# One base for a pair of edge tiles and an untyped first block, in a relational graph layer

## The chip, the cores and the metric

The kernel runs on one core of a Trainium2 chip. The metric is device microseconds (us) of one execution. Three runs of the kernel before took 2129.83 to 2131.13 us, median 2130.83 us. The profiled execution took 2129.83 us.

## The reference

A residual block: rows are normalized and rectified, each edge carries the row of its source through the weight matrix of its type, and the results are summed by destination.

```python
h = jnp.maximum(_layernorm(x, axis=-1), 0.0)          # x: 12500 x 256
hx = jnp.einsum('ni,rio->rno', h, weight)             # 8 types, 256 x 256 each
msg = hx[edge_type, src]                              # 212500 edges
agg = jax.ops.segment_sum(msg, dst, num_segments=num_nodes)
out = x + agg * 0.5**0.5 + h_bias + (h @ loop_weight) * 0.5**0.5
```

The edges are sorted by destination, stably, from 100000 random pairs taken in both directions followed by 12500 self loops. So the last edge of every node is its self loop, and it has a random type like all others.

## The kernel before, in words

The kernel sums before it multiplies. For each node and each of the 8 types it adds up the rows h of the sources (`acc`, a ring of 6 slots of 128 nodes in SBUF, transposed: features on partitions, in two halves of 128 features), and then multiplies each 128 nodes, a *group*, by the eight weights and the loop weight (16 + 2 products, L808, two PE instructions each as the data are f32). There are 98 groups.

**Tiles.** A *unit* is a run of consecutive edges that lies in one partition of a block; a block has 128 units. In the kernel before a unit has 267 edges (`EDGES`). The last edge of each node is taken out of it by five compaction steps on VectorE (L338, L339), which leaves at most 256, two *tiles* of 128. There are 796 units, 1592 tiles and 7 blocks. GpSimd issues one indirect gather for each tile (L637): 128 source rows of 1 KB, from x for the first tiles (their rows are then normalized on the spot, the `e_` lines), from the stored h (`h32`) later. VectorE builds a one-hot matrix for four tiles at once (L650): edge by (node in a window, type). The window is 14 nodes (`WIN`), so 112 columns for a tile. TensorE multiplies (L674, 2 halves x 2 instructions for a tile), VectorE adds the 128 x 224 result to `acc` at a column that a register holds (L684, `add_sums`, one for each tile). Each tile has its own base, hence its own register and its own add.

**Last edges.** They come back by type: for each node the type of its last edge is found (`mark`, `find_types`, `spread_types`), and `begin(g)` writes, for each of the 8 types, the node's own transposed row where the type agrees and zero where it doesn't (8 instructions of L704). That also clears the slot of the ring. `begin` of the groups 0 to 5 stands in the first stage, in `norm_rows`; of the others in `finish` of the group that had the slot before.

**Order.** It is written out by hand. The loop over tiles t issues in each step the gather of tile t + 58 (`AHEAD`), pieces of the normalization of x to h32 in the first 28 or so steps (26 pieces, 4 before the loop, three in four steps), one-hots for later tiles, the edge products of t, steps of `background` work, group products by a budget, and the adds one unit late (`LAG`). Message buffers hold 62 tiles (`MSGS`). `prepare(b)` makes the indices, columns and offsets of block b; its some 70 VectorE instructions go to `background` from step 256 b - 300 on (`PREP`), three list entries (`OPS`) for every 3 steps (`STEP`). All engines run their queues in order. In the last block, which is not full, `load_indices` fills `nat_d` by an iota on GpSimd (L306) before the edges are loaded into it by SP, so this iota stands in GpSimd's queue behind the gather of tile t + 58, and VectorE's first step of the block (L348) waits for the load.

Of the kernel before, what the change touches and what calls it, by code (L numbers as in the profile page):

```python
# [31 lines left out]
WIN = 14  # L32
# [3 lines left out]
SLOTS = 6  # L36
RING = GROUP * SLOTS
# [3 lines left out]

# [19 lines left out]
PREP = 300  # L61
STEP = 3
# [5 lines left out]
class Plan:  # L68
# [5 lines left out]

    def __init__(self, N, E):
        U = EDGES / PAIR
        self.NU = NU = -(-E // EDGES)
        self.NT = NT = NU * PAIR - (1 if E - (NU - 1) * EDGES <= P else 0)
        slack = 6.5 * (E / 4) ** 0.5 / U + 1.0
        self.rate = rate = E / (N * U)  # L80

        self.low = [(1 / rate, -slack / rate), (1.1 / rate, -(2.0 + 0.1 * E / U) / rate)]
        self.high = [(1 / rate, slack / rate)]
        self.starts = list(range(0, N, GROUP))
        self.ends = self.starts[1:] + [N]
        self.NG = len(self.starts)
        self.last = [
            min([NT - 1, *(int((e + 2 - b) / a) + 1 for a, b in self.low)]) for e in self.ends]

        self.last = [min(NT - 1, t + (PAIR - 1 - t) % PAIR) for t in self.last]  # L90
        self.last[-1] = NT - 1

        a, b = self.high[0]
        self.blocks = [
            [k for k in range(-(-NU // P))
             if max(f * PAIR * P * k + o for f, o in self.low) <= e + 2
             and a * PAIR * min(NU - 1, P * k + P - 1) + b + WIN + LASTS + 2 >= s]
            for s, e in zip(self.starts[::XG], self.starts[XG::XG] + [N])]
        a, b = self.high[0]
        self.first = [max(0, int((s - WIN - 2 - b) / a) - 1) if s else 0 for s in self.starts]  # L100

# [101 lines left out]
def kernel(  # L203
# [16 lines left out]
    C = R * WIN  # L220
    assert PAIR * KC * C <= 512
# [5 lines left out]
    EU = E - (NU - 1) * EDGES  # L227
# [18 lines left out]
    low = const.tile([P, NB * PAIR], F32, name="low")  # L246
    high = const.tile([P, NB * PAIR], F32, name="high")
# [4 lines left out]
    ones_b = const.tile([P, P], BF16, name="ones_b")  # L252
    flag = const.tile([1, 1], I32, name="flag")
# [8 lines left out]
    with ExitStack() as main:  # L262
# [11 lines left out]

        selves = main.enter_context(tc.tile_pool(name="selves", bufs=SLOTS + 1))
        marks = main.enter_context(tc.tile_pool(name="marks", bufs=1))
# [14 lines left out]
        added, begun = {}, set()  # L291
# [3 lines left out]
        def load_indices(b):  # L295
            rows_ = min(P, NU - b * P)
            last = b == NB - 1
            full = rows_ - last
            e0 = b * P * EDGES
            nat = {}  # L300
            for name, a, more in (("s", src, 0), ("d", dst, 1), ("t", etype, 0)):
                n = ep.tile([P, EDGES + more], I32, name=f"nat_{name}")
                if last:

                    if more:
                        nc.gpsimd.iota(  # L306
                            n, pattern=[[2, EDGES + 1]], base=N - 2 * EU, channel_multiplier=0)
                    else:
                        nc.vector.memset(n, 0)
                if full:  # L310
                    nc.sync.dma_start(n[:full, :], bass.AP(
                        tensor=a.tensor, offset=a.offset + e0, ap=[[EDGES, full], [1, EDGES + more]]))
                if last:
                    nc.sync.dma_start(
                        n[full : full + 1, :EU], a[E - EU : E].rearrange("(p q) -> p q", p=1))
                nat[name] = n
# [17 lines left out]
        def compacted(got, bit, bits):  # L334

            def step(k):
                m = work_tile(got, "moves", 6, I32)
# [6 lines left out]
        def sources(b, got):  # L344


# [15 lines left out]
            def codes():  # L362
                nc.vector.scalar_tensor_tensor(
                    got["code"], got["code"], float(R), got["t"], op0=ALU.mult, op1=ALU.add)

            def packs():
                nc.vector.scalar_tensor_tensor(
                    packed, got["s"], float(1 << (TB + SB)), got["code"],
                    op0=ALU.mult, op1=ALU.add)

            def unpacks():
                nc.vector.tensor_single_scalar(
                    work_tile(got, "from", 6, I32)[:, :U], packed[:, :U], TB + SB,
# [11 lines left out]
        def last_edges(b, got):  # L385

            def selves_():
                nc.vector.tensor_tensor(
                    work_tile(got, "same", 4), got["s"], got["d"][:, :EDGES], op=ALU.is_equal)

            def ends():
                nc.vector.scalar_tensor_tensor(
                    work_tile(got, "end", 5), got["rise"], 1.0, got["same"],
# [7 lines left out]
            def codes():  # L401
                nc.vector.scalar_tensor_tensor(
                    got["rise"], got["rise"], -2.0 * R, got["t"], op0=ALU.mult, op1=ALU.add)
# [12 lines left out]
            def kept():  # L416
                nc.vector.tensor_single_scalar(
                    work_tile(got, "kinds", 6, I32)[:, :LASTS], packed[:, :LASTS], 2 * R - 1,
# [19 lines left out]
        def columns(b, got):  # L438


            two = slice(b * PAIR, (b + 1) * PAIR)

            def begins():
                got["begin"] = small.tile([P, PAIR], F32, name="begin")
                nc.vector.tensor_copy(got["begin"][:, 0:1], firsts[b])
                more = small.tile([P, 1], I32, name="more")
                nc.vector.tensor_single_scalar(
                    more, got["rest"][:, P : P + 1], TB, op=ALU.logical_shift_right)
                nc.vector.tensor_tensor(got["begin"][:, 1:2], firsts[b], more, op=ALU.add)

            def bases():
                got["base"] = small.tile([P, PAIR], F32, name="base")
                nc.vector.tensor_tensor(got["base"], got["begin"], low[:, two], op=ALU.max)
                nc.vector.tensor_tensor(got["base"], got["base"], high[:, two], op=ALU.min)

            def offs():
                got["off"] = small.tile([P, 1], F32, name="off")
                nc.vector.tensor_tensor(got["off"], firsts[b], got["base"][:, 0:1], op=ALU.subtract)
                got["add"] = small.tile([P, PAIR], F32, name="add")
                nc.vector.tensor_scalar(  # L460
                    got["add"], got["base"], firsts[b], float(-R), op0=ALU.subtract, op1=ALU.mult)
                nc.vector.tensor_scalar(got["add"], got["add"], 1.0, None, op0=ALU.add)
# [15 lines left out]
            def moved():  # L478
                work_tile(got, "col", 2)
                for i in range(PAIR):  # L480
                    h = slice(i * P, (i + 1) * P)
# [4 lines left out]
            def to():  # L486
                nc.vector.scalar_tensor_tensor(
                    got["there"][:, :U], got["col"][:, :U], float(C), got["there"][:, :U],
                    op0=ALU.is_le, op1=ALU.mult)
# [19 lines left out]
            return [begins, bases, offs, fits, number, there, moved, to, final, valid, sum_, all_,  # L509
                    *turned(got, "col", lambda: col.setdefault(b, cols.tile([P, U], F32, name="cols")))]  # L510

        def places(b, got):

            def wraps_():
                got["wrapped"] = small.tile([P, PAIR, NK], F32, name="wrapped")
                for i in range(PAIR):
                    nc.vector.tensor_scalar(
                        got["wrapped"][:, i, :], wraps, got["base"][:, i : i + 1], None,
                        op0=ALU.is_lt)

            def turns():
                got["turns"] = small.tile([P, PAIR], F32, name="turns")
                nc.vector.tensor_reduce(got["turns"], got["wrapped"], AX.X, ALU.add)

            def position():
                got["pos"] = small.tile([P, PAIR], F32, name="pos")
                nc.vector.scalar_tensor_tensor(
                    got["pos"], got["turns"], float(-RING), got["base"], op0=ALU.mult, op1=ALU.add)

            def turn():  # L530
                pt = ps_d.tile([P, 512], F32, tag="pt", name="ptr")
                for i in range(PAIR):
                    nc.tensor.transpose(
                        pt[0:1, i * P : (i + 1) * P], got["pos"][:, i : i + 1], ident)
                place[b] = small.tile([1, U], I32, name="offs")
                nc.vector.tensor_copy(
                    place[b].rearrange("o (u i) -> o i u", i=PAIR),
                    pt[0:1, :U].rearrange("o (i u) -> o i u", i=PAIR))
# [71 lines left out]
        def norm_rows(i):  # L610
# [4 lines left out]
            def rest():  # L615
                after()
                nc.sync.dma_start(rows_of(h32, i), xt[:n, :k, :])
                for g in range(d // P, min(d // P + k, SLOTS, plan.NG)):
                    begin(g, xt[:, g - d // P, :])
# [38 lines left out]
        def load_offsets(t0):  # L658
            n = min(REGS, NT - t0)
            b, q = divmod(t0, U)  # L660
# [3 lines left out]
            for i, v in enumerate(vals):  # L664
                offsets[t0 + i] = v

        def edge_sums(t):
            m, o = msg.pop(t), oh.pop(t)
            if t % PAIR == 0:
                bank = ps_e.tile([P, 512], F32, name="ps")  # L670
                sums["ps"] = bank[:, : PAIR * KC * C].rearrange("p (i c k) -> p i c k", i=PAIR, c=KC)
            ps = sums["ps"][:, t % PAIR]
            for c in range(KC):
                nc.tensor.matmul(ps[:, c], m[:, c * P : (c + 1) * P], o, start=True, stop=True)  # L674
# [5 lines left out]
        def add_sums(t, ps):  # L680
            a = acc[:, :, :, bass.ds(offsets.pop(t), WIN)]
# [3 lines left out]
            added[t] = i.ins  # L685

            assert all(g in begun for g in range(plan.NG) if plan.first[g] <= t)


        def begin(g, rows_):  # L690

            n = plan.ends[g] - plan.starts[g]
            pst = ps_d.tile([P, 512], F32, tag="pt", name="pst")
# [4 lines left out]
            got["self", g] = selves.tile([P, KC, GROUP], F32, name="self_t")  # L698
            copy = nc.scalar.activation(got["self", g][:, :, :n], pst[:, :, :n], AF.Copy)  # L699
            q, k = divmod(g, XG)  # L700
            of = typed[q][:, k * GROUP : k * GROUP + n].unsqueeze(1).to_broadcast([P, KC, n])
            s0 = g % SLOTS * GROUP
            for r in range(R):
# [3 lines left out]
                if r == 0:  # L707
                    tc.add_manual_dep(i.ins, copy.ins.name, SYNC_DEP, reason="one reader at a time")
            begun.add(g)
# [347 lines left out]
```

## Time and profile before

| what | value |
|---|---|
| profiled execution, span and time | 2128.1 us, 2129.83 us |
| median of three runs | 2130.83 us |
| busy: PE, DVE, POOL, ACT | 1642.2, 1475.9, 1515.6, 202.5 us |
| first gather, first edge product | 12.87 us, 81.86 us |
| last gather, last group product ends | 2098.2 us, 2123.1 us |
| first gather from h32 | 189.28 us |
| weights scaled by ACT | 194.8 and 198.7 us, 1.91 us each |
| mean granted clock of TensorE | 0.892 |

How to read it: PE is TensorE's products, DVE is VectorE, ACT is ScalarE, POOL is GpSimd, SP the queue of plain transfers. A view by groups has, after the count, the time in which such instructions ran, the mean of one in ns, and the idle time of the engine ahead of them with what ended it. In views by window the first number is the window's length in us; behind the engines stand the granted clock, the DMA engines' mean busy share and GB/s. A wait is told for the engine that stood still and for what it waited for.

### The profile page before, as it was taken

The numbers are of one execution on the slowest core, as the hardware profiler recorded it, in microseconds if no ns is written. First come the engines' busy times: TensorE is split into PE (matmuls) and PEld (weight loads), VectorE is DVE, ScalarE is ACT, GpSimd is POOL, SyncE is SP. The second block draws the span as 40 slices with busy tenths as digits, with TensorE's granted clock in tenths as the row PEclk, the third lists the DMA queues.
The fourth block names the chain that finished last, engine by engine and source line by source line (L and its number), as shares of the span: only waits on it lengthen the run. The fifth ranks groups of instructions, "written<-read, shape, count | busy, mean of one in ns | idle before, by whom it ended". The sixth has DMA issues, their size and how long they took to land.

```text
span 2128.1 us, 31245 instructions
## 1 busy us (share of the span) xinstructions
PE 1642.2 (77%) x10433; PEld 1497.1 (70%) x10433; DVE 1475.9 (69%) x4268; ACT 202.5 (10%) x473; POOL 1515.6 (71%) x1619
## 2 busy tenths in 40 slices
PE   1134799879999379998389998489999058999999
PEld 0123789769888369887379887378888047888897
DVE  7787887887777387776387776387776067777863
ACT  1465410000000000000000000000000000000000
POOL 6723677777777777777777777777777766777773
PEclk9855899989999699999699999699999578999999
DMA  4786344344434344434344434344344334434442
GB/s 132 234 278 200 87 135 144 105 134 136 135 106 143 104 135 135 137 105 142 105 135 134 131 110 142 105 135 136 106 134 137 104 95 122 135 107 134 131 119 67
DMA packets 145838, 279.32 MB, mean 131 GB/s; under 512 B 27924, under 2 KB 94732, under 8 KB 145676
## 3 DMA queue, kind: packets, MB, share of 16 engines
q0 software_dynamic: 76416, 208.77, 33.7%
q1 hardware_dynamic: 69260, 68.53, 10.1%
q8 instruction: 85, 1.39, 0.3%
q14 instruction: 77, 0.63, 0.1%
HBM read 251.59 MB, written 25.60 MB: 130 GB/s over the span
## 4 chain that ended last, share of the span: by engine, by line
PE 62%; DVE 17%; issue 10%; POOL 4%; DMA 3%; ACT 2%; DVEq 1%; SPq 0%; ACTq 0%; POOLq 0%
PE po L808 33%; PE ps L674 28%; DVE acc L704 5%; POOL msg L637 4%; DVE acc L684 3%; DMA msg<-h,gidx 2%; DVE moves L338 1%; DVE e_stats L585 1%; ACT xt L597 1%; PE pst L696 1%; DVE fixed L339 1%; DVE n_stats L585 1%; DVE oh L650 1%; ACT self_t L699 1%; PE ptt L731 1%
## 5 line engine op out<-in xcount | busy, mean ns | idle before, releaser
L637 POOL DMA_INDIRECT msg<-h,gidx x1496 | 1421.1, 950 | 489.6 <-issue 413.9
L674 PEld LDWEIGHTS ps<-oh,msg 128*128 128x128 f32 x6368 | 960.3, 201 | 372.1 <-issue 179.9
L674 PE MATMUL ps<-oh,msg 128*128 128x112 f32 x6368 | 961.2, 283 | 272.3 <-issue 96.3
L808 PE MATMUL po<-w,acc 128*128 128x256 f32 x3136 | 922.8, 398 | 0.8 <-DVE flag L551 0.8
L684 DVE TENSOR_TENSOR acc<-acc,ps 128x224 f32 x1592 | 613.1, 385 | 122.6 <-PE ps L674 77.3
L808 PEld LDWEIGHTS po<-w,acc 128*128 128x128 f32 x3136 | 529.5, 199 | 26.7 <-issue 0.8
L650 DVE TENSOR_TENSOR oh<-fixed,cols 128x448 f32<-128x448 f32 x398 | 246.8, 620 | 204.5 <-PE ps L674 173.0
L704 DVE SCALAR_TENSOR_TENSOR acc<-types,pst 128x256 f32<-128x256 bf16 (+1 forms) x784 | 267.7, 414 | 63.2 <-ACT self_t L699 60.2
L699 ACT ACTIVATE self_t<-pst 128x256 f32<-128x256 f32 x98 | 37.5, 382 | 1533.5 <-PE pst L696 1533.5
L637 POOL DMA_INDIRECT msg<-in_x_dram,gidx x96 | 92.2, 960 | 93.2 <-issue 57.3
L808 PE MATMUL po<-wl,self_t 128*128 128x256 f32 x392 | 119.6, 434 | 0.0
L808 PEld LDWEIGHTS po<-wl,self_t 128*128 128x128 f32 x392 | 75.4, 214 | 7.4
L731 PE MATMUL ptt<-loops,mark 128*128 128x24 bf16 x272 | 11.4, 178 | 85.8 <-DVE acc L704 83.6
L731 PEld LDWEIGHTS <-mark 128*128 128x128 bf16 x272 | 9.0, 100 | 95.2 <-DVE acc L704 89.2
L326 DVE CAST gidx<-ptr 128x256 int32<-128x256 f32 x7 | 2.9, 420 | 103.5 <-DMA msg<-h,gidx 101.1
L696 PE MATMUL pst<-ident,hr 128*128 128x128 f32 (+1 forms) x184 | 35.9, 278 | 35.4 <-DVE gidx L326 33.9
L348 DVE TENSOR_TENSOR rise<-nat_d 128x267 f32<-128x267 int32 x7 | 3.0, 433 | 79.7 <-DMA nat_d<-in_dst_dram 79.7
L597 ACT ACTIVATE xt<-xt,n_shift,n_rstd 128x256 f32<-128x256 f32 x98 | 51.0, 589 | 29.2 <-DVE n_shift L594 29.2
L597 ACT ACTIVATE msg<-msg,e_shift,e_rstd 128x256 f32<-128x256 f32 x96 | 49.7, 588 | 20.5 <-DVE e_shift L594 18.6
L696 PEld LDWEIGHTS pst<-ident,hr 128*128 128x128 f32 (+1 forms) x184 | 23.6, 151 | 35.8 <-DVE gidx L326 34.0
L819 DVE TENSOR_TENSOR xr<-xr,po 128x256 f32<-128x256 f32 x98 | 40.4, 412 | 8.2 <-PE po L808 7.4
L338 DVE TENSOR_SCALAR moves<-fixed 128x267 int32<-128x267 int32 x98 | 42.3, 432 | 2.1
(209 smaller groups left out, 459.9 us busy)
## 6 DMA issues: line engine op xcount, KB each, us to landing
msg<-h,gidx POOLq DMA_INDIRECT x1496, 2.7
xt<-in_x_dram SPq DMA_DIRECT2D x24, 512.0 KB
h<-xt SPq DMA_DIRECT2D x24, 512.0 KB
xr<-in_x_dram SPq DMA_DIRECT2D x24, 512.0 KB
out_dram<-xr SPq DMA_DIRECT2D x24, 512.0 KB
hr<-h SPq DMA_DIRECT2D x23, 512.0 KB
w<-in_L_gnn_weight_dram SPq DMA_DIRECT2D x2, 1024.0 KB
msg<-in_x_dram,gidx POOLq DMA_INDIRECT x96, 2.8
```

What stands on the lines that cost most here:

```text
L338: nc.vector.tensor_single_scalar(m, packed, 1 << (bit + k), op=ALU.bitwise_and)
L585: nc.vector.bn_stats(stats[:n, j, :], rows_[j])
L597: nc.scalar.activation(rows_[j], rows_[j], AF.Relu, bias=shift[:n, j : j + 1], scale=rstd[:n, j : j + 1])
L637: nc.gpsimd.indirect_dma_start(out=msg[t], out_offset=None, in_=table[:, :], in_offset=bass.IndirectOffsetOnAxis(ap=gidx[b][:, at : at + 1 ...
L650: nc.vector.tensor_tensor(o[:, k : k + v, :i, :], iota_f.unsqueeze(1).unsqueeze(1).to_broadcast([P, v, i, C]), of.unsqueeze(3).to_broadcas ...
L674: nc.tensor.matmul(ps[:, c], m[:, c * P : (c + 1) * P], o, start=True, stop=True)
L684: i = nc.vector.tensor_tensor(a, a, ps, op=ALU.add)
L696: nc.tensor.transpose(pst[:, c, :n], rows_[:n, c * P : (c + 1) * P], ident[:n, :n])
L699: copy = nc.scalar.activation(got["self", g][:, :, :n], pst[:, :, :n], AF.Copy)
L704: i = nc.vector.scalar_tensor_tensor(acc[:, :, r, s0 : s0 + n], of, float(r + 1), pst[:, :, :n], op0=ALU.is_equal, op1=ALU.mult)
L731: nc.tensor.matmul(pt[:, g, :], m[:, i, g * GROUP : (g + 1) * GROUP], loops[b][:, i, :], start=(b, m, i) == parts[0], stop=(b, m, i) == pa ...
L808: i = nc.tensor.matmul(got["out", g][:n], lhs, rhs, start=(r == R and c == 0), stop=(r == R - 1 and c == KC - 1))
```

## The change

- **First block.** Its units have 256 edges and keep all of them, self loops too. So its `sources` needs no compaction, it has no `last_edges`, and its columns come from the destinations themselves (`plain` and so on). The other blocks are as before, 267 edges in a unit. There are 802 units and 1603 tiles.
- **Groups of the first block.** The first three groups of four (`typed` = 3, so groups 0 to 11) lie in it wholly. For them no types are found and `begin` is not called: ScalarE clears the slot (`clear`, 2048 columns of zero), three slots ahead of the loop, three from `background`, the next six in `finish`; the node rows that the loop weight needs are turned later, when the group's turn comes (`turn_nodes` from a re-load of h32).
- **One base for a unit.** The window is 22 nodes for the unit; the first tile's one-hot reaches columns 0 to 22 of it (176 columns with the types), the second's 4 to 22 (144 columns). Both tiles add into one result in PSUM, 352 wide, and one add and one register serve the unit. One-hots are 176 wide for both tiles (704 for four).
- **Background.** `PREP` is 184 for 300 and `STEP` 2 for 3: block b is prepared from step 256 b - 184 on, three entries for every 2 steps. No block is prepared early; block 1 had begun at step 0.
- **Plan.** Due times are counted in units, by the two slopes of edges to units; an add waits for the clearing of a slot that it is the first to reach (`zeroed`).

```diff
-WIN = 14
+WIN = 22
+REACH = ((0, 22), (4, 18))
-PREP = 300
-STEP = 3
+PREP = 184
+STEP = 2
...
         def sources(b, got):
+            if b == 0:
+                def copy():
+                    nc.vector.tensor_copy(work_tile(got, "sf", 2)[:, :U], got["s"][:, :U])
+
+                return [copy, *turned(
+                    got, "sf", lambda: gidx.setdefault(b, idx.tile([P, U], I32, name="gidx")))]
...
         def last_edges(b, got):
+            if b == 0:
+                return []
...
-            return [begins, bases, offs, fits, number, there, moved, to, final, valid, sum_, all_,
+            if b == 0:
+                return [
+                    bases, plain, plain_from, plain_to, plain_typed, plain_final, plain_sum, *turned(
+                        got, "col", lambda: col.setdefault(b, cols.tile([P, U], F32, name="cols")))]
+            return [bases, offs, fits, number, there, moved, to, final, valid, sum_, all_,
...
             def rest():
                 after()
                 nc.sync.dma_start(rows_of(h32, i), xt[:n, :k, :])
-                for g in range(d // P, min(d // P + k, SLOTS, plan.NG)):
-                    begin(g, xt[:, g - d // P, :])
                 load_rows(i + ROWS - 2)
...
-                sums["ps"] = bank[:, : PAIR * KC * C].rearrange("p (i c k) -> p i c k", i=PAIR, c=KC)
-            ps = sums["ps"][:, t % PAIR]
+                sums["ps"] = bank[:, : KC * R * WIN].rearrange("p (c k) -> p c k", c=KC)
+            ps = sums["ps"]
+            i = t % PAIR
+            from_, width = (a * R for a in REACH[i])
+            end = t == NT - 1 or i == PAIR - 1
             for c in range(KC):
-                nc.tensor.matmul(ps[:, c], m[:, c * P : (c + 1) * P], o, start=True, stop=True)
+                nc.tensor.matmul(
+                    ps[:, c, from_ : from_ + width], m[:, c * P : (c + 1) * P], o[:, :width],
+                    start=(i == 0 and c == 0), stop=(end and c == KC - 1))
...
-        def add_sums(t, ps):
-            a = acc[:, :, :, bass.ds(offsets.pop(t), WIN)]
+        def add_sums(u, ps):
+            a = acc[:, :, :, bass.ds(offsets.pop(u), WIN)]
...
+        def clear(g):
+
+            s0 = g % SLOTS * GROUP
+            a = acc[:, :, :, s0 : s0 + GROUP].rearrange("p c r d -> p (c r) d")
+            i = nc.scalar.activation(a, zero.unsqueeze(2).to_broadcast([P, KC * R, GROUP]), AF.Copy)
+            zeroed[g, "slot"] = i.ins
+
+        def turn_nodes(g, pool):
 
             n = plan.ends[g] - plan.starts[g]
+            rows_ = got["h", g // XG][:, g % XG, :]
...
+        def begin(g):
+
+            n = plan.ends[g] - plan.starts[g]
             q, k = divmod(g, XG)
+            pst, copy = turn_nodes(g, selves)
...
                 if b < plan.NG:
-                    begin(b, got["h", b // XG][:, b % XG, :])
+                    if q < plan.typed:
+                        clear(b)
+                    else:
+                        begin(b)
...
-            background = []
-            early = {0}
-            for q in range(-(-min(SLOTS, plan.NG) // XG)):
-                for b in plan.blocks[q]:
-                    if b not in early:
-                        early.add(b)
-                        for f in prepare(b):
-                            f()
-                mark(q)
-                find_types(q)
-                spread_types(q)
+            for g in range(min(CLEARED, plan.NG)):
+                clear(g)
+
+            background = [(4 * (g - CLEARED), lambda g=g: clear(g))
+                          for g in range(CLEARED, min(SLOTS, plan.NG))]
...
                 for b in range(1, NB):
-                    if t == max(0, U * b - PREP) and b not in early:
+                    if t == max(0, U * b - PREP):
...
-                waiting.append((t, ps))
-                while waiting and (
-                        t == NT - 1 or t % PAIR == PAIR - 1 and len(waiting) > LAG * PAIR):
-                    for i in range(min(PAIR, len(waiting))):
-                        u, ps = waiting.pop(0)
-                        add_sums(u, ps)
+                if t % PAIR == PAIR - 1 or t == NT - 1:
+                    waiting.append((t // PAIR, ps))
+                while waiting and (len(waiting) > LAG or t == NT - 1):
+                    u, ps = waiting.pop(0)
+                    add_sums(u, ps)
```

## The prediction

> **What bounds the kernel now.** First the page's slices (span in 40, so 53.2 us each).
>
> ```profile
> PE   1134799879999379998389998489999058999999
> POOL 6723677777777777777777777777777766777773
> PEclk9855899989999699999699999699999578999999
> ```
>
> POOL shows 7 nearly throughout, while PE has holes, some down to 3 and one to 0. So the even engine is POOL, though no engine looks full. Next the groups, to see what POOL does, and the prices of what the change touches.
>
> ```profile
> L637 POOL DMA_INDIRECT msg<-h,gidx x1496 | 1421.1, 950 | 489.6 <-issue 413.9
> L674 PE MATMUL ps<-oh,msg 128*128 128x112 f32 x6368 | 961.2, 283 | 272.3 <-issue 96.3
> L684 DVE TENSOR_TENSOR acc<-acc,ps 128x224 f32 x1592 | 613.1, 385 | 122.6 <-PE ps L674 77.3
> L650 DVE TENSOR_TENSOR oh<-fixed,cols 128x448 f32<-128x448 f32 x398 | 246.8, 620 | 204.5 <-PE ps L674 173.0
> L704 DVE SCALAR_TENSOR_TENSOR acc<-types,pst 128x256 f32<-128x256 bf16 (+1 forms) x784 | 267.7, 414 | 63.2 <-ACT self_t L699 60.2
> ```
>
> A gather is 0.95 us and is followed by 0.30 us that nothing else explains. That is a cadence, and the gathers by window show it.
>
> ```profile
> 82.00:188.00 106.00, 39.37 (x42) 0.55 0.79 254
> 188.00:266.00 78.00, 42.76 (x46) 0.78 0.44 136
> 266.00:1640.00 1374.00, 1040.45 (x1096) 0.93 0.43 127
> ```
>
> From 266 to 1640 us POOL issued 1096 gathers in 1374 us, 1.25 each: it never stopped, and PE's holes there cost nothing. Before that it stopped: all 62 buffers were full while the normalization went on. Its lost time until the last block's iota: 1295 gathers stand ahead of that, 12.9 + 1295 x 1.25 = 1632, and the iota starts at 1714.2, so 82 us: by 188 us (97 gathers) 54, from 188 to 266 (46 gathers) 20, and 8 later.
>
> Then what happens at that iota (VectorE's and POOL's order of time).
>
> ```profile
> 1645.01 0.28 DVE L309 MEMSET nat_t<- 128x267 int32 x1
> 1716.46 0.44 DVE L348 TENSOR_TENSOR rise<-nat_d 128x267 f32<-128x267 int32 x1 [71.17 <-DMA nat_d<-in_dst_dram]
> ```
>
> ```profile
> 1714.22 0.37 POOL L306 IOTA nat_d<- 128x268 int32 x1
> ```
>
> PE had caught up with the gathers, VectorE reached step 1236 and then stood 71 us, because POOL's iota stands behind the gather of tile 1294. All engines but POOL stand with it. After it PE is the bound: 350 tiles (1242 of 1592 are done) end at 2123.1. From 1800 to 2100 the edge products count 1144, so 286 tiles in 300 us, 1.049 each; 350 x 1.049 = 367, and the other 40 of the 407 us are 25 in 1716 to 1800 (224 products, 56 tiles, in 84 us, block 6 being prepared) and 15 at the end. So the end is: **POOL's time to the iota, then PE's time for the tiles left.**
>
> **The change part by part.**
>
> *First gather.* 17 VectorE steps between 3.5 us and the turn of the indices go; a cast of 0.3 us, the turn and its 0.42 us copy stay. 12.9 becomes about 5: -8.
>
> *Ahead of tile 0* (81.9 us now). Gone: these 8; `last_edges` of block 0, 14.5 to 26.1, 11.7; marks and types, 33.8 to 43.4, 9.6; six `begin`, each 4.0 from start to start, 24. Added: three one-hots at 704 (0.62 for 448, at the difference between 224 and 448 wide 0.89), 0.8, and a wider memset 0.3. Three clears of 2048 columns at 1.91 (the weights' scaling, the same width) run on ACT, which was idle there until 36 us. Sum -52: tile 0 at about 31.
>
> *Normalization stage,* 82 to 188 us now, 28 tiles. VectorE was busy 86 of 106 us. It loses block 1's preparation (some 20 of its 24 us) and the wait for its `nat_d`, 6.2; one add of 352 for two of 224 is 0.52 for 0.77 (3 less), one-hots 3 more: 80, an end at 111. But the transfers: 10.7 MB of x, 12.8 MB of h and 71 gathers, 9.3 MB, 32.8 MB in all; 254 GB/s at 0.79 share is 321 at full share, 290 at 0.9: 113 us, an end at 144. I take 140, near the transfers, since both reads and gathers now want them at once. POOL then stands at 28 + 62 = 90 gathers, and could have 135 / 1.25 = 108: 22 us lost, for 54. Bounds: end at 111, none lost; at 155, 37 lost.
>
> *Tiles 28 to 96.* The 20 us lost become 9: the `begin` of groups 6 and up are gone, but block 1's preparation falls in from step 72. Bounds 3 and 20. Later losses 4 for 8. **Sum lost 35** (ends 5 and 65) for 82.
>
> *Steady stage.* An edge product is now 176 or 144 columns. Two rows bound it, from the chain of waits:
>
> ```profile
> 2013.19 1.77 PE ps L674 x16
> 2105.12 3.04 PE po L808 x14
> ```
>
> 112 columns take 111 ns, 256 columns 217. Least: nothing is added (the 112-wide is held by its weight load, not its columns). Most: on the line between, 146 on the mean of the two widths, +35. I take 217 in proportion to the width, 149 and 122, mean 135.5, since two rows at different slopes say that the narrow one has a floor: +24.5 x 4 = 0.098 us for a tile, 1.049 to 1.147. The Trainium skill, "TensorE: Matmul & The Clock Gate", section "LDWEIGHTS (loading the stationary operand)", speaks against this change: a load takes its column count over 1.2 GHz, 107 ns for 128, whatever the product's width. The 111 agrees with it; so up to some 128 columns were free and those above are not. With that page's slope (N over 2.4 GHz plus 2.5, here twice as the f32 row of 217 shows) the mean is 136, and the sum would be the same within 1 us for the tiles that count.
>
> VectorE: adds 802 x 0.52 for 1592 x 0.385, -197 us; one-hots 401 x 0.89 for 247, +109; 12 `begin` less, -33. It isn't the bound, so this is worth nothing by itself; what covers it is PE at 1.05 to 1.15 us a tile. Its share of the add to the tile (0.78 against 0.84) only shortens the catch-up after a preparation. ACT's 12 clears, 23 us, lie in its idle time (202.5 us busy).
>
> Until the iota PE's longer tile is covered by POOL: tile 96 at about 232, 1257 tiles x 1.147 and five preparations at 20 end at 1774. That is before the iota, so it costs nothing; with the cover gone it is a rival.
>
> *The iota's place.* PREP 184 moves it to step 1352, behind gather 1410. What stays queued behind VectorE's wait is the same as before: adds, one-hots, then PE. The wait of the earlier blocks for index buffers goes, as by step 256 b - 184 the gathers of block b - 2 are out; it was covered by POOL and yields nothing. POOL reaches the iota after 1411 gathers: 5 + 1764 + 35 = 1804, and 2 for the load, 1806. That is 92 us later than now.
>
> *After it.* 1603 - 1353 = 250 tiles x 1.147 = 287. The 40 beside: 25 of preparation, now packed in 46 steps, with less VectorE work in a tile, and 15 at the end; I keep 40 (32 to 48). 327 in place of 407.
>
> **Sum.** 1806 + 327 = 2133, and 5 to the span's end as now (2128.1 against 2123.1): 2138. The span now is 2128.1, the execution 2129.8 and the median 2130.8, so add 2.7: about **2140**. In words: 55 us won in the first stage, 116 gathers (145 us) put ahead of the iota, 100 tiles (105 us) fewer behind it, and 25 us of wider products.
>
> **The rivals.**
>
> *Faster.* The first stage is worth more and the width less: normalization ends by 118 (VectorE's bound nearly), lost 12, and PE at 1.09. 5 + 1764 + 12 + 2 + 272 + 40 + 8 = 2103. For it: VectorE, not the transfers, was busiest in that stage (the share of 0.79 has room). Against it: 9.3 MB of gathers no longer wait. It decides below a normalization end of 125.
>
> *PE the bound throughout (slower).* At the line's price PE needs 1.19 a tile, and 25 for a preparation: 232 + 1507 x 1.19 + 150 + 15 + 8 = 2198. It decides once PE reaches step 1352 after 1806, at 1.17 a tile. Then POOL's buffers are full all along and no wait shows at the iota. Against: POOL's 1.25 leaves it room.
>
> *The early start buys nothing.* Transfers hold the normalization until 175 us: lost 77, 2182. Against: VectorE's 86 of 106 us busy in that stage.
>
> **How the numbers follow.** The forecast 0.58, its own range 2118 to 2162; faster 0.24; PE-bound 0.12; early start in vain 0.06. A difference under 0.2%, 4.3 us, can't be told from none here. The forecast gives faster 0.08, same 0.11, slower 0.39; the faster rival 0.23 and 0.01; the other two 0.18 slower. Together faster 0.31, same 0.12, slower 0.57. The range takes the lost time's ends (5 to 65) and the tile's (1.049 to 1.19), not both at once: 2102 to 2182.
>
> **What will show it.** First gather near 5 us, tile 0 near 31, first gather from h near 142; POOL 1.25 a gather from some 250 us on; an iota near 1804 with VectorE standing 20 to 70 us at the first step of block 6; edge products of 16 in a row some 2.2 us; after the iota 1.15 a tile. It would be wrong if POOL's gathers slow down beside the normalization, if no wait shows at the iota, or if PE's tile stays at 1.05.

## The result and the profile after

| | before | after |
|---|---|---|
| median of 4 runs each | 2130.33 us | 2106.9 us |
| profiled execution, span and time | 2128.1, 2129.83 us | 2105.2, 2107.2 us |
| first gather, first edge product | 12.87, 81.86 us | 4.80, 26.44 us |
| first gather from h32 | 189.28 us | 125.0 us |
| iota of the last block | 1714.22 us | 1782.61 us |
| last group product ends | 2123.1 us | 2100.2 us |
| mean granted clock of TensorE | 0.892 | 0.924 |

The ratio is 0.9893, with a 95% interval of 0.9862 to 0.9923: some 23 us less, where 10 more were forecast. The slices of the changed kernel's page (52.6 us each):

```profile
PE   2468999998999998999988998988998860799998
POOL 7767777777777777777777777777777777677750
PEclk8578999998999999999999999999999985899999
```

POOL has no weak slices at the start any more. PE's start, 1 1 3 4 before, is 2 4 6 8, and its dips to 3 in mid-run are gone. The hole of 0 at the last block's iota stands, two slices later. The gathers from h (and x) by window, the window's length in us first, then POOL's busy time and count on that line, the clock, the DMA share and GB/s:

```profile
26.00:106.00 80.00, 60.47 (x64) 0.58 1.06 371
106.00:180.00 74.00, 50.08 (x53) 0.81 0.58 176
180.00:266.00 86.00, 63.65 (x69) 0.92 0.44 128
266.00:1714.00 1448.00, 1096.36 (x1155) 0.96 0.43 126
```

64 gathers in 80 us is the full cadence of 1.25 us, and 1155 in 1448 us is nearly 1.25 again, three gathers short. Only from 106 to 180 us does POOL fall behind by more: 53 instead of 59. The groups that answer to those of the kernel before:

```profile
L683 POOL DMA_INDIRECT msg<-h,gidx x1507 | 1430.0, 949 | 481.7 <-issue 396.3
L723 PE MATMUL ps<-oh,msg 128*128 128x176 f32 (+1 forms) x6412 | 1146.2, 310 | 187.5 <-DVE acc L735 76.6
L735 DVE TENSOR_TENSOR acc<-acc,ps 128x352 f32 x802 | 412.9, 515 | 180.9 <-PE ps L723 171.9
L696 DVE TENSOR_TENSOR oh<-fixed,cols 128x704 f32<-128x704 f32 x402 | 356.0, 886 | 356.2 <-PE ps L723 349.3
L773 DVE SCALAR_TENSOR_TENSOR acc<-types,pst 128x256 f32<-128x256 bf16 (+1 forms) x688 | 234.8, 414 | 74.5 <-ACT self_t L762 73.0
```

Half as many adds at 515 ns take 200 us less, the wider one-hots 109 more, and 96 instructions of `begin` are gone: VectorE's three terms are as they were taken. The edge products (L723) are busy for 185 us more. What happens at the last block's iota, in VectorE's and POOL's order of time (start, duration, instruction, and in brackets the idle time ahead of it):

```profile
1710.22 0.28 DVE L320 MEMSET nat_t<- 128x268 int32 x1
1784.86 0.44 DVE L366 TENSOR_TENSOR rise<-nat_d 128x267 f32<-128x267 int32 x1 [74.36 <-DMA nat_d<-in_dst_dram]
```

```profile
1781.65 0.95 POOL L683 DMA_INDIRECT msg<-h,gidx  x1 [0.30 <-issue]
1782.61 0.37 POOL L317 IOTA nat_d<- 128x268 int32 x1
```

VectorE stands 74 us, three more than before, behind the gather of tile 1410, which ends as the iota starts. From there PE is the bound. Its part in the chain that ended last, and the edge products' PE, weight load and VectorE time in a window of that stretch:

```profile
1981.61 2.17 PE ps L723 x16
```

```profile
1850.00:2075.00 225.00, 137.98 (x805) 128.88 (x804) 51.67 (x101) 0.98 0.36 104
```

Sixteen products in a row take 2.17 us, 136 ns each. 805 products are 201 tiles in 225 us: 1.118 us a tile.

The two spans differ by three rows alone. POOL lost 14 us ahead of the iota (1782.6 less 4.8 and 1411 x 1.25) for 82, and began 8 earlier: -76. It had 116 more gathers ahead of the iota: +145. From the iota to the last group product it is 315 + 2 us for 407 + 2: 245 tiles at 1.118 for 350 at 1.049, -92. In all -23.

### The profile page after: what moved, and what is told of

The parts are those of the page before. It is cut to its first block, busy times and chain, and to the rows that moved or that the text cites. A ratio compares the mean times of both kernels' runs of the same rounds, so it can differ in the third digit from the quotient of the medians.

```text
span 2105.2 us, 29382 instructions
## 1 busy us (share of the span) xinstructions
PE 1789.1 (85%) x10411; PEld 1644.1 (78%) x10411; DVE 1327.7 (63%) x3274; ACT 218.5 (10%) x470; POOL 1523.2 (72%) x1630
## 4 chain that ended last, share of the span: by engine, by line
PE 67%; DVE 13%; issue 6%; DMA 6%; POOL 4%; ACT 2%; SPq 0%; DVEq 0%; ACTq 0%; POOLq 0%
PE ps L723 34%; PE po L883 31%; DMA msg<-h,gidx 4%; POOL msg L683 4%; DVE acc L773 3%; DVE acc L735 2%; DVE moves L349 2%; DVE fixed L350 2%; DMA h<-xt 1%; ACT xt L645 1%; DVE oh L696 1%; PE pst L759 1%; DMA w<-in_L_gnn_weight_dram 1%; DVE n_stats L633 0%; PE ptt L800 0%
## 5 line engine op out<-in xcount | busy, mean ns | idle before, releaser
L723 PE MATMUL ps<-oh,msg 128*128 128x176 f32 (+1 forms) x6412 | 1146.2, 310 | 187.5 <-DVE acc L735 76.6
L723 PEld LDWEIGHTS ps<-oh,msg 128*128 128x128 f32 x6412 | 1056.2, 198 | 290.1 <-issue 100.9
L883 PE MATMUL po<-w,acc 128*128 128x256 f32 x3136 | 892.7, 387 | 0.0
L696 DVE TENSOR_TENSOR oh<-fixed,cols 128x704 f32<-128x704 f32 x402 | 356.0, 886 | 356.2 <-PE ps L723 349.3
L883 PEld LDWEIGHTS po<-w,acc 128*128 128x128 f32 x3136 | 547.4, 195 | 25.3
L735 DVE TENSOR_TENSOR acc<-acc,ps 128x352 f32 x802 | 412.9, 515 | 180.9 <-PE ps L723 171.9
L773 DVE SCALAR_TENSOR_TENSOR acc<-types,pst 128x256 f32<-128x256 bf16 (+1 forms) x688 | 234.8, 414 | 74.5 <-ACT self_t L762 73.0
L894 DVE TENSOR_TENSOR xr<-xr,po 128x256 f32<-128x256 f32 x98 | 40.4, 412 | 7.4 <-PE po L883 7.4
L895 DVE TENSOR_TENSOR xr<-xr,po 128x256 f32<-128x256 f32 x98 | 41.2, 421 | 3.4
L818 ACT ACTIVATE diagonal<-ident,kinds 128x128 bf16<-128x128 f32 x88 | 28.1, 390 | 113.8 <-DVE kinds L815 113.8
L759 PE MATMUL pst<-ident,hr 128*128 128x128 f32 x196 | 37.7, 274 | 0.4 <-DVE offs L586 0.2
```

The lines of the kernel that those rows point to most:

```text
L696: nc.vector.tensor_tensor(o[:, k : k + v, :i, :], iota_f.unsqueeze(1).unsqueeze(1).to_broadcast([P, v, i, C]), of.unsqueeze(3).to_broadcas ...
L723: nc.tensor.matmul(ps[:, c, from_ : from_ + width], m[:, c * P : (c + 1) * P], o[:, :width], start=(i == 0 and c == 0), stop=(end and c == ...
L735: i = nc.vector.tensor_tensor(a, a, ps, op=ALU.add)
L759: nc.tensor.transpose(pst[:, c, :n], rows_[:n, c * P : (c + 1) * P], ident[:n, :n])
L773: i = nc.vector.scalar_tensor_tensor(acc[:, :, r, s0 : s0 + n], of, float(r + 1), pst[:, :, :n], op0=ALU.is_equal, op1=ALU.mult)
L883: i = nc.tensor.matmul(got["out", g][:n], lhs, rhs, start=(r == R and c == 0), stop=(r == R - 1 and c == KC - 1))
```

## The experiments

Every kernel was timed against runs of the kernel before on the same chip. The changed kernel itself was timed in the comparison above alone.

**First series.** The theory was that of the prediction, with the lost time put right: POOL to the iota, then PE. If so, the iota's wait and the width of the products are what the change still pays for. The rivals were that the earlier preparation sets the end, or that PE's products do all along. The iota was taken off POOL in both kernels: VectorE computes the same line from one that it has.

```diff
-                        nc.gpsimd.iota(
-                            n, pattern=[[2, EDGES + 1]], base=N - 2 * EU, channel_multiplier=0)
+                        nc.vector.tensor_scalar(
+                            n, line[:, : EDGES + 1], 2.0, float(N - 2 * EU),
+                            op0=ALU.mult, op1=ALU.add)
```

On the changed kernel:

> The changed kernel with the last block's filling of nat_d computed by VectorE from a row of numbers that it has, instead of the iota in GpSimd's queue. Theory (the end is POOL's time to the iota plus PE's time after it): the 74 us wait goes, POOL's last gather comes near 4.8 + 1603 x 1.25 + 14 = 2023, and PE, only some ten tiles behind the gathers, ends 20 to 30 us later: about 2050 (2040 to 2065). Rival (the wait only moves, to the load of the block or to its preparation): 2090 to 2107.

On the kernel before:

> The same edit in the kernel before. Theory: there POOL's own time is nearly the end, as its first stage lost it 82 us: the last gather stays near 2085 to 2095 and the end comes near 2113, 15 to 20 us less than before. Rival (the wait costs its 71 us in both kernels): about 2060.

`PREP` 300 and `STEP` 3 again, in the changed kernel:

> The changed kernel with PREP and STEP as before (300 and 3). Theory: the iota stands behind 1295 gathers and not 1411, 145 us earlier, and 116 more tiles come after it, 130 us at 1.118; block 1's preparation is back in the normalization stage and costs POOL 5 to 20: 2095 to 2110, much like the changed kernel. Rival (the later preparation is itself the gain, by its freed index buffers): 2125 or more.

A window of 14 nodes in it, so products of 112 columns and adds of 224 (`WIN = 14`, `REACH = ((0, 14), (0, 14))`, and the flag for the general path never set):

> The changed kernel with a window of 14 nodes for the unit and both tiles' products 112 columns wide; edges outside it are left out, and the branch to the general path is never taken. Theory (width counts only after the iota): iota unchanged near 1783, then a tile of about 1.03 for 1.118, 245 tiles: 2080 to 2090. Rival (the wider products are hidden, as TensorE's other products got quicker): 2100 to 2107. Rival (width counts everywhere): below 2060.

No expectation in us can be judged by this series: on its chip the kernel before itself took 2584.2 us. The four took 2577.85, 2586.69, 2589.69 and 2554.13 us: ratios 0.9974 (0.9954 to 0.9994), 1.0011 (0.9991 to 1.0031), 1.0007 (0.9977 to 1.0038) and 0.9893 (0.9862 to 0.9924). The changed kernel without the iota shows why, in its slices and the head of its chain of waits:

```profile
PE   0248887877878778777887787787788788787788
POOL 7435666666566656565666566566666666665640
```

```profile
PE 52%; another core or an unknown queue 23%; DVE 13%; issue 9%; ACT 2%; DMA 1%; DVEq 0%; SPq 0%; ACTq 0%
```

POOL shows 5 and 6 in place of 7: it waits, and the longest of the waits that the view can name is for PE's edge products, which free the message buffers (us in all, times, longest):

```profile
POOL msg L684 <- PE ps L724: 253.3, 123, 9.1
```

PE nowhere reaches 9, and 23% of the chain is time whose releaser the trace doesn't hold; where that comes from stays open. PE, with these waits in its chain, holds POOL up all along there, as in the rival of PE as the bound. Only the edit that shortens PE's work, the width, moved the time by more than 0.3% from the kernel before. Taking the iota off POOL was worth nothing in the kernel before; what it was worth in the changed one can't be said, as that kernel has no time on this chip.

**Second series, the kernel before at 2129.8 us.** The same three edits, and a fourth:

> The changed kernel without the iota in GpSimd's queue, again, as in the first series the kernel before itself took 2584 us, with pauses of TensorE that its profile of 2128 us doesn't have. If the kernel before takes about 2130 here: theory 2050 (2040 to 2065), the rival (the wait only moves) 2090 to 2107. If it takes about 2580 again: TensorE is the bound all along and this is within 0.5% of it.

It took 2049.39 us, ratio 0.9623 (0.9607 to 0.9639), as expected, and beats both kernels: 57 us less than the changed one's 2106.9. Its slices, and its gathers by window:

```profile
PE   2468999997999997999897988997899988899898
POOL 7767777777777777777777777777777777777773
```

```profile
266.00:1714.00 1448.00, 1096.13 (x1156) 0.96 0.43 126
1714.00:2020.00 306.00, 231.40 (x245) 0.96 0.42 123
```

PE's hole is gone, and POOL issues to 2020 us at 1.25 a gather. The VectorE wait at the first step of the last block is 3.4 us there. So POOL is the bound from its first gather to the last, but for some 13 us that it lost, most of them before 180 us; 26 us follow behind it.

> The kernel before without the iota in GpSimd's queue, again. With the kernel before at about 2130: theory 2113 (last gather 2085 to 2095), rival (the wait costs its 71 us in both) 2060.

It took 2112.94 us, 0.9918 (0.9902 to 0.9935), as expected. In the kernel before the wait was worth 17 us only, in the changed one 57. The later place of the iota, behind 116 more gathers, is one part of that, and the wider products behind it are another: with `PREP` 300 and `STEP` 3 in the changed kernel the wait is worth 34.5 us (2106.4 less 2071.87, both below), and with the window of 14 nodes 32.4 (2078.54 less 2046.1; the kernel before differs by 1.3 us between these two series). Between the two kernels without the iota lie 63.6 us. That is POOL's account within 2 us: 76 us won at the start, less 11 more gathers, 14 us.

> The changed kernel with a window of 14 nodes and both products 112 columns wide (edges outside are left out, the general path's branch never taken), again. With the kernel before at about 2130: theory (width counts only after the iota) iota near 1783, end 2080 to 2090; rival (hidden) 2100 to 2107; rival (width counts everywhere) below 2060. With it at about 2580: some 1.1% below it, as in the first series.

It took 2078.54 us, 0.976 (0.9743 to 0.9776), just below what was expected. The iota came at 1778.75 us, 4 us earlier than with the wide products, and behind it the same 245 tiles took 288.8 us for 315.3. So 26.5 of the 30.3 us between the two profiled spans lie after the iota: the width costs there and hardly anywhere else. The narrower window shortens VectorE's one-hots and adds too; the products alone, four in a tile at 149 or 122 ns against 112 (the medians given further down), make 23 us of it by estimate.

The fourth edit does one part of the change alone, on the kernel before: the first groups' types and `begin` give way to clears on ScalarE (this leaves out the last edges of nodes 0 to 767).

```diff
-                    begin(g, xt[:, g - d // P, :])
+                    begin(g, xt[:, g - d // P, :], False)
...
-                mark(q)
-                find_types(q)
-                spread_types(q)
+            for g in range(min(SLOTS, plan.NG)):
+                s0 = g * GROUP
+                nc.scalar.activation(
+                    acc[:, :, :, s0 : s0 + GROUP].rearrange("p c r d -> p (c r) d"),
+                    zero.unsqueeze(2).to_broadcast([P, KC * R, GROUP]), AF.Copy)
+            background += [(12, lambda: mark(1)), (14, lambda: find_types(1)), (20, lambda: spread_types(1))]
...
```

> The kernel before with its first six groups cleared by ScalarE in place of their six begins and of the first group of marks (the second group's marks come from background at steps 12 to 20); the last edges of nodes 0 to 767 are left out. Theory (POOL's lost time ahead of the iota decides the end one for one): tile 0 some 33 us earlier, near 49, normalization's end and the first gather from h 25 to 35 earlier, and the end with them: 2095 to 2105 where the kernel before takes 2130. Rival (the normalization stage takes up what is won, as its transfers are at their limit): 2120 to 2130.

It took 2101.5 us, 0.9868 (0.9852 to 0.9885), as expected. Its gathers by window:

```profile
82.00:188.00 106.00, 49.86 (x53) 0.52 0.81 260
188.00:266.00 78.00, 51.66 (x55) 0.91 0.36 103
```

53 and 55 gathers for 42 and 46: POOL's lost time until the iota falls from 82 to 57 us, the iota comes 25 us earlier, and the run is 28 us shorter. The first edge product came at 53.2 us and the first gather from h at 164.1. So of the early start the missing types and `begin` give about a third; what the uncompacted first block and the later preparation of block 1 give of the rest was not taken apart.

**Third series, the kernel before at 2128.47 us.** First the change's background pace: undone in the changed kernel, and done alone in the kernel before.

> The changed kernel with PREP and STEP as before (300 and 3), again. With the kernel before at about 2130: theory (POOL's time to the iota plus PE's after it): iota at 4.8 + 1295 x 1.25 + 14 to 30 = 1638 to 1654, 361 tiles at 1.118 and 41 after it, end 2092 to 2108, within 15 of the changed kernel's 2107. Rival (the later preparation is itself the gain): 2125 or more.

> The kernel before with PREP 184 and STEP 2, nothing else. With the kernel before at about 2130: theory: the iota behind 1411 gathers, 12.9 + 1764 + 65 to 80 lost = 1842 to 1857, then 234 tiles at 1.049 and 40: end 2132 to 2152, slower than before. Rival (no more waits for index buffers, so faster): 2115 or less.

Undone it gave 2106.4 us, 0.99 (0.9872 to 0.9929), the changed kernel's own time. The iota came 125 us earlier, at 1657.1, but the end didn't: POOL had lost 33.5 us (the expectation had 14 to 30) and PE had the more tiles behind the iota. Done alone it gave 2145.48 us, 1.0085 (1.0061 to 1.0109), 17 us slower, the iota at 1852.4. Both totals fell where they were expected. So a later iota was worth nothing by itself in these kernels: it costs a gather's 1.25 us for each tile of about 1.05 to 1.12 us that it spares PE behind it.

Then the width and the pace once the iota is off POOL, to see whether their price follows the bound.

> The changed kernel without the iota in GpSimd's queue and with both products 112 columns wide (edges outside the window of 14 nodes are left out, the general path's branch never taken). Theory (POOL is then the pacemaker to the end): last gather near 2018, end 2042 to 2049, at most 7 less than the 2049.4 without the iota, where the width was worth 28 with the iota. Rival (width costs its 0.1 us on every tile that TensorE runs behind): 2035 or less.

2046.1 us, 0.9617 (0.9594 to 0.964), as expected, and 3.3 us less than with wide products. Its last gather stands at 2020.2 us, as theirs. The 28 us of width are 3 once POOL is the bound to the end.

> The changed kernel without the iota in GpSimd's queue and with PREP 300, STEP 3. Theory: block 1 is prepared in the normalization stage, which costs POOL up to 15 us there; waits for index buffers come back but POOL runs on over them: 2049 to 2065. Rival (the index-buffer waits hold the end): 2070 or more.

2071.87 us, 0.9737 (0.9713 to 0.9761): a miss, 7 us above the theory's upper end and within what the rival had. The rival's mechanism was that VectorE's waits for index buffers hold POOL near the end. VectorE's waits and POOL's gathers by window in this kernel:

```profile
DVE gidx L338 <- DMA msg<-h,gidx: 112.9, 4, 33.0
```

```profile
106.00:180.00 74.00, 32.99 (x36) 0.63 0.59 186
266.00:1714.00 1448.00, 1096.51 (x1154) 0.94 0.43 126
```

and with the new pace, the first of these windows:

```profile
106.00:180.00 74.00, 51.38 (x56) 0.82 0.57 176
```

The waits are there, 112.9 us of them, but from 266 to 1714 us POOL issues 1154 gathers for 1156: they cost it nothing. The loss is 20 gathers, 25 us, between 106 and 180 us, and the last gather is 26 us later. At the old pace block 1's preparation lies in the normalization: VectorE's first step of it comes at 39.6 us, after a wait of 10.7 us for the block's load, and the last store of h is issued at 134.0 us for 111.9 with the new pace. So the theory had the place and not the price, which it took as up to 15 us. The new pace is worth some 22 us without the iota, and with it nothing.

## Why the prediction was wrong in its sign

**The failed step** is POOL's lost time in the sum, and in it the 22 us of the normalization stage: "I take 140, near the transfers". The stage ended at 112 us and cost POOL nothing. The step took 321 GB/s for the full rate of the transfers, from 254 at a share of 0.79, and then nine tenths of that. The stage in the changed kernel, with all engines (PE, its weight loads, VectorE, ScalarE, POOL's gathers):

```profile
26.00:106.00 80.00, 36.23 (x125) 32.37 (x126) 62.38 (x285) 67.04 (x140) 60.47 (x64) 0.58 1.06 371
```

371 GB/s, at a "share" of 1.06. A share above 1 can only be a sum of packet times that overlap, so dividing by it gave no capacity. The kernel before shows as much: in its own stage, 82 to 188 us, in 40 slices of 2.65 us, the transfers come to 390 and 400 GB/s where they are thick.

```profile
GB/s 259 390 400 180 148 257 334 395 389 312 315 376 283 186 215 180 221 244 385 294 276 330 363 261 184 269 293 351 299 214 250 164 275 171 76 221 187 160 0 61
```

So the transfers weren't the end of that stage; VectorE's queue was. From 26 to 111 us VectorE waits for ScalarE's answers within the normalization, and once for something that the view doesn't name, but for no transfer that it names (us in all, times, longest):

```profile
DVE n_rstd L641 <- ACT n_rstd L637: 11.9, 15, 1.8
DVE n_rstd L641 <- issue: 3.6, 1, 3.6
DVE e_rstd L641 <- ACT e_rstd L637: 2.0, 6, 0.3
```

And with the old background pace, which puts block 1's preparation back into VectorE's queue there, the last store of h is issued at 134.2 us for 113.0 (10.9 us of it VectorE's wait for the block's load), while the transfers from 26 to 106 us run at 335 GB/s for 371. How near to a limit of their own they run at 371 isn't shown. VectorE's own bound of 111 us, worked out in the same step and kept as the lower end, is near what came: its last statistics step starts at 110.1 us and its last normalization step at 112.2. That is in part luck, as the stage began 4.6 us before the 31 us it was worked out from and took 86 us for 80. POOL issued a gather every 1.25 us all the while, and the first gather from h, the 97th, stands at 125.0 (142 predicted). The point that was named as deciding for the faster rival, a normalization end below 125, was met; that rival's sum, 2103, is 4 us from the median.

**The lost time** follows. Taken as 22 + 9 + 4 = 35 us, it measured 14: none by 106 us, some 8 from there to 180, and 6 in the 1600 us behind that. That is 21 of the 33 us between the predicted span of 2138 and 2105.2; it puts the iota at 1782.6, predicted 1804.

**After the iota** 12 us more. 245 tiles were left for 250, as PE had run five tiles ahead of VectorE's step: 6 us. The widths were taken rightly: the median from one product's start to the next is 149 ns for 176 columns, 122 to 123 for 144 and 112 for 112, so the choice of the proportional price over the line between two rows held. The other 6 us aren't taken apart. By the windows a tile cost 1.118 us for 1.147, but about half of that is where the windows are cut. PE's long waits in them (1800 to 2100 us before, 1850 to 2075 us after) are those behind VectorE's `begin`, and they come in pieces of 3.3 to 3.6 us, once in about 70 us:

```profile
PE ptt L731 <- DVE acc L704: 13.5, 4, 3.6
PE ptt L800 <- DVE acc L773: 6.6, 2, 3.3
```

Four of them fell into 286 tiles, two into 201: 47 ns a tile against 33. PE's busy time is firmer: 285.95 us for the 286 tiles and 218.38 for the 201, so 1.000 and 1.085 us a tile, 85 ns more where 98 were put. What makes the 13 ns no run shows. One figure of the prediction, on which nothing rests, is off: the mean of 136 ns by the slope of the page that it names is 138 when the whole slope is doubled, some 3 us in the sum where it says 1.

**What held.** The mechanism, POOL's time to the iota and then PE's time for the tiles left, gave the kernels of the second and third series their places within a few us, but for the one miss above. The first gather (4.80 for 5), the first edge product (26.4 for 31), the wait at the iota (74, just above "20 to 70") and POOL's unchanged 1.25 us a gather held too. That VectorE's shorter work is worth nothing by itself was not tried alone. The rival of PE as the bound throughout failed here (1.118 is below its 1.17); it is what the chip of the first series showed.

**Where the expected gain went.** 76 us of POOL's time were won, 14 go to 11 more gathers, and some 40 are given back at the iota, where the changed kernel pays 57 us for the wait, with its later place and the wider products behind it, and the kernel before 17.

## What to carry to other kernels

When two bounds of a stage lie 30 us apart, a transfer rate that was measured while something else held the stage is no capacity: look for the slices in which the transfers are thickest (400 GB/s here, where the mean was 254), take the engine's bound as the likeliest, and let the transfers widen the range. An operation on an engine that issues transfers ahead in order costs what is queued before it, here 57 us for a 0.37 us iota; look for such ones before weighing the widths and paces around them. What an edit is worth changes with the bound: 28 or 3 us for the same width, 22 or 0 for the same pace.

## What the runs showed of the hardware

A wide product behind narrow ones ran late, and the narrow one behind wide ones made up for it. PE's order of time in the kernel before, and in the changed one (start, duration of the group, count):

```profile
1892.33 0.59 PE L674 MATMUL ps<-oh,msg 128*128 128x112 f32 x4
1892.76 0.61 PE L808 MATMUL po<-w,acc 128*128 128x256 f32 x2
1893.21 0.59 PE L674 MATMUL ps<-oh,msg 128*128 128x112 f32 x4
```

```profile
1955.17 0.65 PE L723 MATMUL ps<-oh,msg 128*128 128x144 f32 x4
1955.66 0.59 PE L883 MATMUL po<-w,acc 128*128 128x256 f32 x2
1956.10 0.76 PE L723 MATMUL ps<-oh,msg 128*128 128x176 f32 x4
1956.69 0.59 PE L883 MATMUL po<-w,acc 128*128 128x256 f32 x2
```

Where a wide product follows a narrow one, the next product starts 232 ns after it in the kernel before (the median of 1140 cases, behind 112 columns) and 216 ns after it in the changed one (behind 144 or 176); with the window of 14 nodes it is 232 again. But a 112-column product that follows a wide one has its successor after 96 ns in place of 112 (the median of 1269 cases). So a round of four narrow and two wide products takes 878 ns (the median of 772; 1892.33 to 1893.21 is one), no more than 4 x 112 + 2 x 216 = 880: nothing is lost by the order. Why it is shifted so, no run here shows.

The kernel before took 2584.2 us on the chip of the first series, and 2129.8 and 2128.47 us on the chip of the second and third. The variants of the first series took 474 to 528 us longer on the first than on the other, and the one shown above has waits in its chain that the trace gives no releaser for.
